# Layer 0's attention: the last four blocks of every second unit's weights turned over on TensorE instead of VectorE

## The chip, the cores and the metric

One core of one Trainium2 chip runs the whole kernel. The metric is device time in microseconds (us), the median of several executions. One more execution was taken with the hardware profiler on; its own time stands beside the others below, and all durations of single instructions come from it.

## The reference, cut to what matters

The kernel computes four layers on an input of 2 x 256 x 32 x 32. Only layer 0 is touched. After a group normalisation it is

```python
q = conv1x1(xn, Wq, bq); k = conv1x1(xn, Wk, bk); v = conv1x1(xn, Wv, bv)   # (2, 32, 32, 256)
qf = q.reshape(8192, 64) / sqrt(64)      # 2048 positions x 4 heads
kf = k.reshape(8192, 64); vf = v.reshape(8192, 64)
A = softmax(qf @ kf.T, axis=1)           # 8192 x 8192: heads share all keys
O = (A @ vf).reshape(2, 32, 32, 256)
x = x + O @ Wo.T + bo
```

All numbers are fp32. Every one of the 8192 queries attends to all 8192 keys, so the matrix of weights is large and never stored. Layers 1 to 3 (another attention, a windowed attention, additive attention, two mixtures of experts) follow and are the same before and after.

## The kernel before, in words

`layer0` normalises, computes `qT`, `kT` and `v`, and calls `shared_attention`. There 64 **rows** are run, each of 32 positions with their 4 heads. A row has 4 **units**: unit `m` belongs to row `i = m // 4`, to the pair of heads `p = m // 2 % 2` and to the half `h = m % 2` of the keys. An odd unit therefore has `h = 1`.

A unit passes through these steps, each a small function:

- `score(m)` (line 143): 16 matmuls (32 in the records, since an fp32 matmul shows as two) into two PSUM tiles, `ps_s0` (two buffers) and `ps_s1` (one buffer). The 128 partitions are 4 groups `c` of 32 queries. The 1024 columns are 32 blocks `b` of 32 keys `i`: partition group `c` and column block `b` meet in the 32 keys `(b, c, i)`. VectorE copies the first tile to `sc0` with a running minimum (line 150, the "eviction" below), ScalarE the second to `sc1` (line 153).
- `fold` (lines 166 to 168, GpSimd) and `reduce` (line 172, VectorE) find the minimum of `sc1`; a gather by DMA (line 159), `spread_least` (line 178 on VectorE) and four more DMAs (line 181) bring each query's minimum to all partitions as `sa_shift`.
- `weigh(m)` (line 188, ScalarE): two exponentials over 128x1024, in place in `sc0` and `sc1`.
- `turn(m)` (line 201, VectorE): two stream transposes over 128x1024. Each turns every 32x32 block on its own, so that in the tile `wt` a block's 128 keys `(c, i)` stand on the partitions and 32 queries in the columns.
- `value(m)` (line 211, TensorE): 16 matmuls (32 records) that multiply `wt` by the rows of `v` and sum into `ps_o`, which has one buffer and holds one row.

At the end of a row `invert`, `spread` (line 230: one matmul into `ps_n`, copied to `norm` by ScalarE, line 235) and `done` (line 372: VectorE multiplies `ps_o` by `norm` into `oT`) normalise it. Every eighth row `done` also runs the output projection, 8 matmuls (16 records) into `ps_out` (line 379), and adds it to `x` on VectorE (line 386). `ps_n` and `ps_out` share one PSUM buffer, the tag `ps_t` of the pool `p_t`.

The order is written out by hand, under `tc.manual_schedule()`: the program order of each engine is the order of the calls. Iteration `n` of the loop calls `reduce(n-2)`, the row's `done`, `turn(n-7)`, `spread_least`, `weigh(n-6)`, `score(n)`, `fold(n)`, the rest of `done` (the projection), `invert`, `spread`, `value(n-10)`, each where its unit or row exists. Engines run freely within that order and meet at semaphores. `sc0` has 7 buffers, so the eviction of unit `n` writes where unit `n-7` stood; `sc1` has 8, `wt` 3.

```python
for n in range(units + 15):
    ...
    if on(7):
        turn(n - 7)
```

Of the kernel before, what the change touches and what calls it, by code (L numbers as in the profile page):

```python
# [19 lines left out]
F32 = mybir.dt.float32  # L20
# [3 lines left out]
ALU = mybir.AluOpType  # L24
# [3 lines left out]
P = 128  # L28
B, C, N = 2, 256, 1024
T = B * N  # L30
NT = T // P
# [38 lines left out]
class Stack:  # L70
# [34 lines left out]

    def shared_attention(self, qT, kT, v, ctx, done):

        tc, nc = self.tc, self.nc
        S, G, B = 32, P // 32, N // 32
        rows = T // S
        units = 4 * rows
        psum = lambda name, bufs: ctx.enter_context(tc.tile_pool(name=name, bufs=bufs, space=PSUM))
        p_a, p_b, p_o, p_t = psum("sa_a", 2), psum("sa_b", 1), psum("sa_o", 1), psum("sa_t", 1)
        sb = ctx.enter_context(tc.tile_pool(name="sa_sb", bufs=2))
        keys = kT.rearrange("p n (b c i) -> p n b c i", c=G, i=S)
        ones = sb.tile([S, P], F32, name="ones", bufs=1)
        nc.gpsimd.memset(ones, 1.0)  # L130
        names = "least folded got shift total parts scores weights sums rec norm"
        least, folded, got, shift, total, parts, scores, weights, sums, rec, norm = ({} for _ in names.split())

        def score(m):
            i, p, h = m // 4, m // 2 % 2, m % 2
            if h == 0:
                least[m // 2] = self.small.tile([P, 2, 2], F32, name="sa_least")
            ps = [pool.tile([P, 2, CH], F32, name=f"ps_s{r}") for r, pool in enumerate((p_a, p_b))]
            for a in range(2):
                for c in range(G):  # L140
                    for r in range(2):
                        half = slice(64 * r, 64 * r + 64)
                        nc.tensor.matmul(  # L143
                            ps[r][S * c : S * (c + 1), a, :].rearrange("p (b i) -> p b i", i=S),
                            lhsT=qT[half, p, S * i : S * (i + 1)], rhs=keys[half, 2 * h + a, :, c, :],
                            start=True, stop=True,
                        )
            scores[m] = [sb.tile([P, N], F32, name=f"sc{r}", bufs=7 + r) for r in range(2)]
            flat = [x.rearrange("p a b -> p (a b)") for x in ps]
            nc.vector.tensor_scalar(  # L150
                scores[m][0], flat[0], 1.0, None, ALU.mult, ALU.min, accum_out=least[m // 2][:, 0, h : h + 1]
            )
            nc.scalar.copy(scores[m][1], flat[1])  # L153

        def gather(t, n, name, engine=nc.sync):

            g = self.small.tile([S, n, G, 2], F32, name=name)
            for c in range(G):
                engine.dma_start(out=g[:, :, c, :], in_=t[S * c : S * (c + 1)])
            return g.rearrange("q n c h -> q n (c h)")  # L160

        def fold(m):
            x = scores[m][1]
            a, b = x[:, :CH], x[:, CH:]
            folded[m] = y = sb.tile([P, CH], F32, name="fold")
            nc.gpsimd.tensor_tensor(y, a, b, ALU.subtract)  # L166
            nc.gpsimd.tensor_scalar(y, y, 3.0e38, 0.0, ALU.min, ALU.max)
            nc.gpsimd.tensor_tensor(y, a, y, ALU.subtract)  # L168

        def reduce(m):  # L170
            h = m % 2
            nc.vector.tensor_reduce(least[m // 2][:, 1, h : h + 1], folded.pop(m), AX.X, ALU.min)
            if h == 1:
                got[m // 2] = gather(least.pop(m // 2), 2, "sa_got")

        def spread_least(k):
            t = self.small.tile([S, 2], F32, name="sa_min")
            nc.vector.tensor_reduce(t, got.pop(k), AX.X, ALU.min)
            shift[k] = self.small.tile([P, 2], F32, name="sa_shift")
            for c in range(G):  # L180
                nc.sync.dma_start(out=shift[k][S * c : S * (c + 1)], in_=t)

        def weigh(m):
            i, p, h = m // 4, m // 2 % 2, m % 2
            if m % 4 == 0:
                total[i] = self.small.tile([P, 4, 2], F32, name="sa_total")
            for r in range(2):
                nc.scalar.activation(  # L188
                    scores[m][r], scores[m][r], AF.Exp, bias=shift[m // 2][:, r : r + 1], scale=-1.0,
                    accum_out=total[i][:, 2 * p + r, h : h + 1],  # L190
                )
            if m % 4 == 3:

                parts[i] = gather(total.pop(i), 4, "sa_sums", nc.sync if i < rows - 3 else nc.scalar)

        def turn(m):
            i, p, h = m // 4, m // 2 % 2, m % 2
            if p == 0:
                weights[i, h] = sb.tile([P, 4, N], F32, name="wt", bufs=3)
            for r, x in enumerate(scores.pop(m)):  # L200
                nc.vector.transpose(weights[i, h][:, 2 * p + r, :], x)  # L201

        def value(m):
            i, h, j = m // 4, m // 2 % 2, m % 2
            if h == 0 and j == 0:
                sums[i] = p_o.tile([P, 4, S], F32, name="ps_o")
            for t in range(B // 4):
                for k in range(2):
                    b = B // 2 * k + B // 4 * j + t
                    at = B * h + b  # L210
                    nc.tensor.matmul(  # L211
                        sums[i][64 * k : 64 * (k + 1)],
                        lhsT=v[:, at % NT, 64 * (at // NT) : 64 * (at // NT + 1)],
                        rhs=weights[i, h][:, :, S * b : S * (b + 1)],
                        start=(h == 0 and j == 0 and t == 0), stop=(h == 1 and j == 1 and t == B // 4 - 1),
                    )

        def invert(i):
            t, r = (self.small.tile([S, 4], F32, name=f"sa_{n}") for n in ("tot", "rec"))
            nc.vector.tensor_reduce(t, parts.pop(i), AX.X, ALU.add)  # L220
            nc.vector.reciprocal(r, t)
            rec[i] = sb.tile([S, 4, S], F32, name="diag")
            shape = [S, 4, S]
            nc.gpsimd.tensor_tensor(
                rec[i], self.ident[0:S, 0:S].unsqueeze(1).to_broadcast(shape), broadcast(r, shape), ALU.mult
            )

        def spread(i):
            ps = p_t.tile([P, 4, S], F32, name="ps_n", tag="ps_t")
            nc.tensor.matmul(  # L230
                ps.rearrange("p n q -> p (n q)"), lhsT=ones, rhs=rec.pop(i).rearrange("p n q -> p (n q)"),
                start=True, stop=True,
            )
            norm[i] = sb.tile([P, 4, S], F32, name="norm")
            nc.scalar.copy(norm[i], ps)

        with tc.manual_schedule():
            for n in range(units + 15):
                on = lambda d: 0 <= n - d < units
                row = lambda d: on(d) and (n - d) % 4 == 0  # L240
                if on(2):
                    reduce(n - 2)
                if row(14):
                    i = (n - 14) // 4
                    ended = done(i, sums.pop(i), norm.pop(i), p_t)
                    next(ended)
                if on(7):
                    turn(n - 7)
                if on(4) and (n - 4) % 2 == 0:
                    spread_least((n - 4) // 2)  # L250
                if on(6):
                    weigh(n - 6)
                if on(0):
                    score(n)
                    fold(n)
                if row(14):
                    next(ended, None)
                    next(ended, None)
                if row(11):
                    invert((n - 11) // 4)  # L260
                if row(13):
                    spread((n - 13) // 4)
                if on(10):
                    value(n - 10)
# [3 lines left out]
    def layer0(self, xT):  # L268
        tc, nc = self.tc, self.nc
        with ExitStack() as ctx:  # L270
# [4 lines left out]
            qT = big.tile([P, CC, T], F32, name="qT")  # L275
            kT = big.tile([P, 4, T], F32, name="kT")
            v = big.tile([P, NT, C], F32, name="v")

            with tc.tile_pool(name="l0_xn", bufs=1) as xp, tc.tile_pool(
                name="l0_ps", bufs=4, space=PSUM  # L280
# [67 lines left out]
                for i in range(NT):  # L348
# [5 lines left out]
                        )  # L354
                    nc.vector.tensor_tensor(v[:, i, :], ps, bv, ALU.add)


            zero = big.tile([P, C], F32, name="zero")
            nc.gpsimd.memset(zero, 0.0)
# [25 lines left out]
                    x = xT[:, o, t * C : (t + 1) * C]  # L385
                    nc.vector.scalar_tensor_tensor(x, ps[:, o, :], bo[:, o : o + 1], x, ALU.add, ALU.add)

            self.shared_attention(qT, kT, v, ctx, done)

    def pool_stats(self, pool, psum, mv, average, tag="ps_row"):  # L390

# [1445 lines left out]
```

## Time and profile before

| what | value |
|---|---|
| median of 3 runs | 2885.95 us (2885.02 to 2887.11) |
| the profiled execution | 2887.74 us, of which the recorded span 2886.0 us |
| mean granted TensorE clock | 0.967; 1.00 in layer 0's attention |
| layer 0's scores | from 62.15 us to about 1130 us |
| busy in the span: TensorE, VectorE, ScalarE, GpSimd | 91%, 67%, 63%, 43% |
| busy from 200 to 1100 us: VectorE, TensorE | 98% to 100%, 96% to 99% in every 100 us |

An engine's busy time is the time in which at least one of its instructions is in flight. Matmul records overlap each other (the mean record of line 211 lasts 276 ns although 32 of them start within 1.9 us), so for TensorE the distance between starts says more than the busy share. "PEld" are weight loads, which have records of their own. In a list of groups the columns are line, engine, operation, output and input, shapes, count, then busy time and mean duration of one, then the engine's idle time just before and what ended it. In a timeline they are start, duration until the end of the merged instructions, engine, line, operation and count, and in brackets the idle time before with what ended it.

### The profile page before, as it was taken

To read this page: it belongs to the slowest core of one execution; us is meant where nothing else is said; L and a number is where in the kernel's file an instruction comes from. 1 tells how busy PE (TensorE), PEld (TensorE's weight loads), DVE (VectorE), ACT (ScalarE), POOL (GpSimd) and SP (SyncE) were. 2 spreads that over 40 slices of the span, in tenths; PEclk is the share of its full clock that TensorE was granted. 3 is DMA by queue.
4 is the path that set the end of the run, shared out by engine and by line. 5 is a ranking of instruction groups with operands and counts; after the bars stand their busy time and mean duration, and the time that the engine had idled before them with its cause. 6 is when DMAs were issued, how large, how long until landed. Compare 5 with 4: busy or idle time off the path is not lost. (4 is left out here: it accounts for less than half of the span.)

```text
span 2886.0 us, 77396 instructions
## 1 busy us (share of the span) xinstructions
PE 2635.3 (91%) x32006; PEld 1643.6 (57%) x32006; DVE 1944.8 (67%) x3642; ACT 1815.6 (63%) x2685; POOL 1235.5 (43%) x1302
## 2 busy tenths in 40 slices
PE   7899999999999998799999686999999988999987
PEld 3455555555555555555555454998666632465676
DVE  5999999999999999478789577633422343134242
ACT  2777777778777777255555231211699878889722
POOL 4877777777777775001111134244111112102242
PEclk9999999999999999899999897999999999899998
DMA  3000000000000000111010100543222001322354
GB/s 133 3 3 3 3 3 3 3 3 3 3 3 3 3 3 3 49 31 28 11 31 9 28 1 30 202 134 99 68 81 76 16 24 35 128 67 87 116 166 125
DMA packets 180577, 131.39 MB, mean 46 GB/s; under 512 B 130992, under 2 KB 162368, under 8 KB 173056
## 3 DMA queue, kind: packets, MB, share of 16 engines
q0 software_dynamic: 29232, 81.71, 8.5%
q1 hardware_dynamic: 147824, 44.25, 6.8%
q8 instruction: 251, 4.11, 0.6%
q10 hardware_dynamic: 3168, 0.48, 0.1%
q14 instruction: 102, 0.84, 0.1%
HBM read 181.24 MB, written 29.49 MB: 73 GB/s over the span
## 5 line engine op out<-in xcount | busy, mean ns | idle before, releaser
L188 ACT ACTIVATE sc<-sc,sa_shift 128x1024 f32<-128x1024 f32 x512 | 584.5, 1144 | 153.1 <-DMA sa_shift<-sa_min 150.8
L201 DVE STREAM_TRANSPOSE wt<-sc 128x1024 f32<-128x1024 f32 x512 | 601.5, 1207 | 0.2 <-ACT sc L188 0.2
L1622 ACT ACTIVATE th<-kT,qb 128x1024 f32<-128x1024 f32 x512 | 540.4, 1135 | 66.2 <-PE ps_e L1631 40.1
L211 PEld LDWEIGHTS ps_o<-wt,v 128*64 128x64 f32 x8192 | 444.4, 137 | 188.9 <-issue 106.2
L143 PE MATMUL ps_s<-kT,qT 64*32 64x512 f32 x8192 | 527.6, 595 | 18.0 <-ACT sc L153 17.2
L211 PE MATMUL ps_o<-wt,v 128*64 128x128 f32 x8192 | 505.0, 276 | 26.8 <-DVE oT L372 26.7
L166 POOL TENSOR_TENSOR fold<-sc 128x512 f32<-128x512 f32 x256 | 329.2, 1286 | 195.9 <-ACT sc L153 177.0
L168 POOL TENSOR_TENSOR fold<-sc,fold 128x512 f32<-128x512 f32 x256 | 328.4, 1283 | 21.4
L153 ACT COPY sc<-ps_s 128x1024 f32<-128x1024 f32 x256 | 256.0, 1000 | 111.0 <-PE ps_s L143 57.1
L1631 PE MATMUL ps_e<-th,pick 128*32 128x512 f32 x2048 | 305.7, 613 | 20.5 <-ACT th L1622 9.3
L1404 PEld LDWEIGHTS ps_h<-xe,ew 128*128 128x128 f32 x2320 | 278.1, 194 | 63.6 <-issue 39.0
L150 DVE TENSOR_SCALAR_CACHE_REDUCE sc<-ps_s 128x1024 f32<-128x1024 f32 x256 | 304.3, 1189 | 7.1 <-PE ps_s L143 6.6
L1404 PE MATMUL ps_h<-xe,ew 128*128 128x128 f32 x2320 | 295.0, 281 | 13.7 <-issue 5.6
L1424 PE MATMUL ps_y<-ew,h 128*128 128x256 f32 x1160 | 275.6, 387 | 8.2 <-ACT h L1410 5.6
L143 PEld LDWEIGHTS ps_s<-kT,qT 64*32 64x32 f32 x8192 | 134.4, 106 | 230.2 <-issue 163.4
L1424 PEld LDWEIGHTS ps_y<-ew,h 128*128 128x128 f32 x1160 | 215.6, 193 | 66.7 <-issue 23.0
L630 ACT ACTIVATE sc<-sc,l_least 128x1024 f32<-128x1024 f32 x128 | 146.7, 1147 | 125.8 <-DVE sc L617 125.5
L1415 DVE TENSOR_TENSOR hb<-ps_h,ew 128x512 f32<-128x512 f32 x115 | 79.4, 691 | 207.3 <-PE ps_h L1404 167.1
L1428 DVE COPY y<-ps_y 128x256 f32<-128x256 f32 x99 | 41.9, 423 | 229.7 <-PE ps_y L1424 209.9
L1393 ACT ACTIVATE h<-hb 128x512 f32<-128x512 f32 x115 | 71.5, 623 | 193.0 <-DVE hb L1415 173.7
L636 DVE STREAM_TRANSPOSE wt<-sc 128x1024 f32<-128x1024 f32 x128 | 153.3, 1225 | 46.0 <-ACT sc L630 25.4
L617 DVE TENSOR_SCALAR_CACHE_REDUCE sc<-ps_s 128x1024 f32<-128x1024 f32 x128 | 150.7, 1213 | 40.3 <-PE ps_s L609 40.2
(286 smaller groups left out, 3139.1 us busy)
## 6 DMA issues: line engine op xcount, KB each, us to landing
xr<-slots_in SPq DMA_DIRECT2D x99, 128.0 KB
slots_out<-y SPq DMA_DIRECT2D x99, 128.0 KB
sa_got<-sa_least SPq DMA_DIRECT2D x512, 0.5 KB
sa_shift<-sa_min SPq DMA_DIRECT2D x512, 0.2 KB
slots_in<-zero POOLq DMA_DIRECT2D x46, 128.0 KB
kh<-kh SPq DMA_DIRECT2D x32, 128.0 KB
qh<-qh SPq DMA_DIRECT2D x32, 128.0 KB
sa_sums<-sa_total SPq DMA_DIRECT2D x244, 1.0 KB
```

The costliest lines, as they stand in the source:

```text
L143: nc.tensor.matmul(ps[r][S * c : S * (c + 1), a, :].rearrange("p (b i) -> p b i", i=S), lhsT=qT[half, p, S * i : S * (i + 1)], rhs=keys[ha ...
L150: nc.vector.tensor_scalar(scores[m][0], flat[0], 1.0, None, ALU.mult, ALU.min, accum_out=least[m // 2][:, 0, h : h + 1])
L153: nc.scalar.copy(scores[m][1], flat[1])
L166: nc.gpsimd.tensor_tensor(y, a, b, ALU.subtract)
L168: nc.gpsimd.tensor_tensor(y, a, y, ALU.subtract)
L188: nc.scalar.activation(scores[m][r], scores[m][r], AF.Exp, bias=shift[m // 2][:, r : r + 1], scale=-1.0, accum_out=total[i][:, 2 * p + r, ...
L201: nc.vector.transpose(weights[i, h][:, 2 * p + r, :], x)
L211: nc.tensor.matmul(sums[i][64 * k : 64 * (k + 1)], lhsT=v[:, at % NT, 64 * (at // NT) : 64 * (at // NT + 1)], rhs=weights[i, h][:, :, S * ...
L1404: nc.tensor.matmul(ps[:, j, :], lhsT=a[:, c, at : at + P], rhs=x[:, c, :], start=(c == 0), stop=(c == CC - 1),)
L1424: nc.tensor.matmul(ps, lhsT=h[:, j, :], rhs=w2[:, j, :], start=(j == 0), stop=(j == HB - 1))
L1622: nc.scalar.activation(h, keys, AF.Tanh, bias=self.qb[b][:, s // G, g : g + 1])
L1631: nc.tensor.matmul(pe[i][c * U : (c + 1) * U, a, :], lhsT=self.pick[:, k, :], rhs=h[:, a, :], start=(k == 0), stop=(k == G - 1),)
```

## The change

For odd units (`h = 1`) VectorE turns only the first 896 of the 1024 columns of each score tile. The last 128 columns, four blocks of 32, are turned by TensorE in the new step `turn_last(m)`: two transposes of 128x128 (one for `sc0`, one for `sc1`) into one PSUM tile `ps_t`, which has the buffer that `ps_n` and `ps_out` use, and one copy by ScalarE into the columns of `wt` that were left out. In iteration `n` it stands behind `score(n)` and `fold(n)`, and ahead of the projection and of `value(n-10)`.

A transpose of a whole 128x128 puts other keys together than four transposes of 32x32 do: the partitions become `(b, i)` of the last four blocks and the 32-column groups become `c`. So the four matmuls of `value` that take these columns need the rows of `v` in that order. They are computed once in `layer0`, as `v_last`: GpSimd copies the normalised inputs into the order (two copies), 8 matmuls (64 columns each) multiply them by the last 64 columns of `wv`, and VectorE adds the bias. `diag` and `norm` go from two buffers to one.

```diff
+    def turn_last(m):
+        i, p, h = m // 4, m // 2 % 2, m % 2
+        both = scores.pop(m)
+        if h == 0:
+            return
+        ps = p_t.tile([P, 2, P], F32, name="ps_t", tag="ps_t")
+        for r, x in enumerate(both):
+            nc.tensor.transpose(ps[:, r, :], x[:, N - P :], self.ident)
+        nc.scalar.copy(weights[i, h][:, 2 * p : 2 * p + 2, N - P :], ps)
 
     def turn(m):
-        for r, x in enumerate(scores.pop(m)):
-            nc.vector.transpose(weights[i, h][:, 2 * p + r, :], x)
+        n = N - h * P
+        for r, x in enumerate(scores[m]):
+            nc.vector.transpose(weights[i, h][:, 2 * p + r, :n], x[:, :n])
...
     def value(m):
-                    lhsT=v[:, at % NT, 64 * (at // NT) : 64 * (at // NT + 1)],
+                    lhsT=v[:, at % NT, 64 * (at // NT) : 64 * (at // NT + 1)]
+                    if h == 0 or b < B - G else v_last[:, b - (B - G), :],
...
-        rec[i] = sb.tile([S, 4, S], F32, name="diag")
+        rec[i] = sb.tile([S, 4, S], F32, name="diag", bufs=1)
-        norm[i] = sb.tile([P, 4, S], F32, name="norm")
+        norm[i] = sb.tile([P, 4, S], F32, name="norm", bufs=1)
...
                 if on(0):
                     score(n)
                     fold(n)
+                if on(7):
+                    turn_last(n - 7)
...
     # layer0, behind the loop that computes v
+    last = xp.tile([P, CC, 4, 4, 32], F32, name="last")
+    runs = xn[:, :, T - 4 * P :].rearrange("p a (b c i) -> p a b c i", b=4, c=4)
+    for c in range(CC):
+        nc.gpsimd.tensor_copy(last[:, c].rearrange("p c b i -> p b c i"), runs[:, c])
+    ps = psum.tile([P, 4, 64], F32, name="ps_v", tag="ps_row")
+    for t in range(4):
+        for c in range(CC):
+            nc.tensor.matmul(
+                ps[:, t, :], lhsT=last[:, c, t].rearrange("p b i -> p (b i)"), rhs=wv[:, c, C - 64 :],
+                start=(c == 0), stop=(c == CC - 1),
+            )
+    nc.vector.tensor_tensor(v_last, ps, bv[:, C - 64 :].unsqueeze(1).to_broadcast([P, 4, 64]), ALU.add)
```

More of the change, by code (lines that the diff above doesn't have):

```diff
@@ L104, in rsqrt, with shared_attention @@
         return r
-    def shared_attention(self, qT, kT, v, ctx, done):
+    def shared_attention(self, qT, kT, v, v_last, ctx, done):
         tc, nc = self.tc, self.nc
@@ L277, in layer0 @@
             v = big.tile([P, NT, C], F32, name="v")
+            v_last = big.tile([P, 4, 64], F32, name="v_last")
             with tc.tile_pool(name="l0_xn", bufs=1) as xp, tc.tile_pool(
@@ L386, in done @@
                     nc.vector.scalar_tensor_tensor(x, ps[:, o, :], bo[:, o : o + 1], x, ALU.add, ALU.add)
-            self.shared_attention(qT, kT, v, ctx, done)
+            self.shared_attention(qT, kT, v, v_last, ctx, done)
     def pool_stats(self, pool, psum, mv, average, tag="ps_row"):
```

## The prediction

> **What bounds the kernel now.** I read the busy times by stretch first, each stretch one group of 8 rows, from the start of a row's first line-211 matmul to that of the eighth row after it.
>
> ```profile
> 235.80:370.00 134.20, 132.81 (x2082) 77.51 (x2082) 133.53 (x202) 104.55 (x167) 103.35 (x104) 1.00 0.06 3
> ...
> 909.40:1043.90 134.50, 131.56 (x2081) 77.54 (x2080) 133.64 (x202) 105.39 (x168) 104.74 (x105) 1.00 0.06 3
> sum 808.10, PE 790.15 PEld 464.44 DVE 801.63 ACT 633.24 POOL 625.93; mean PE 131.69 PEld 77.41 DVE 133.60 ACT 105.54 POOL 104.32
> ```
>
> Columns: length, then busy time of TensorE, its weight loads, VectorE, ScalarE, GpSimd. VectorE works 133.6 of 134.7 us, so it is the bound; ScalarE and GpSimd have 29 us left. TensorE's 131.7 cannot be taken at its word, since its records overlap. The groups of VectorE in this window come next:
>
> ```profile
> L201 DVE STREAM_TRANSPOSE wt<-sc 128x1024 f32<-128x1024 f32 x384 | 451.1, 1207 | 0.0
> L150 DVE TENSOR_SCALAR_CACHE_REDUCE sc<-ps_s 128x1024 f32<-128x1024 f32 x192 | 228.1, 1188 | 0.5
> L172 DVE TENSOR_REDUCE sa_least<-fold 128x1 f32<-128x512 f32 x192 | 127.3, 663 | 0.0
> ```
>
> The last field is idle time: there is none, and the transposes are the largest part. How much room TensorE has is read from starts in its timeline, the rows around a projection:
>
> ```profile
> 631.12 1.97 PE L211 MATMUL ps_o<-wt,v 128*64 128x128 f32 x32
> 633.01 1.95 PE L143 MATMUL ps_s<-kT,qT 64*32 64x512 f32 x32
> 635.98 3.72 PE L379 MATMUL ps_out<-oT,sb_wo 128*128 128x256 f32 x16 [1.02 <-DVE oT L372]
> 639.63 1.97 PE L211 MATMUL ps_o<-wt,v 128*64 128x128 f32 x32
> 641.53 1.95 PE L143 MATMUL ps_s<-kT,qT 64*32 64x512 f32 x32
> 643.41 1.97 PE L211 MATMUL ps_o<-wt,v 128*64 128x128 f32 x32
> ...
> 650.96 0.48 PE L230 MATMUL ps_n<-diag,ones 32*128 32x128 f32 x2
> 651.37 1.97 PE L211 MATMUL ps_o<-wt,v 128*64 128x128 f32 x32
> ```
>
> Back to back, value costs 1.90 us (639.63 to 641.53), score 1.88 (641.53 to 643.41), `ps_n` 0.41, the projection 3.65. So a row on TensorE alone is 4 x 3.78 + 0.41 = 15.53 (15.51 by the rows' starts), and a group 8 x 15.51 + 3.65 = **127.7 us**. The starts of rows in a quiet group show who leads: 20.25 (with the projection), 15.51, 15.51, 16.52, then 16.60 four times, together 134.2. After a projection VectorE has caught up and TensorE sets the pace for two rows; then VectorE falls behind again, its eviction starting 0.2 us after the scores' end in the first unit and about 3 us after it from the tenth on, and rows take 16.6. TensorE's room is 134.2 - 127.7 = 6.5 us a group. That is all that the new work may use.
>
> **The change, part by part.**
>
> *Off VectorE.* A group has 16 odd units, so 32 shorter transposes. By proportion 128 of 1024 columns are 1207/8 = 151 ns; by the slope between 128x512 (663) and 128x1024 (1188) they are (1188 - 663)/4 = 131 ns, different operations but the same engine. I take 0.133: -4.3 us a group (-4.8 at most). VectorE's floor becomes 133.6 - 4.3 = **129.3**. Were nothing else changed, 64 rows would give 34 us.
>
> *Onto TensorE.* 16 pairs of transposes a group. The same operation on fp32 stands at line 1661, here in front of matmuls on part of the columns (128*32), as it will be in front of value (128*64):
>
> ```profile
> 2210.02 1.09 PE L1661 MATMUL ps_pt<-ident,sc_a 128*128 128x128 f32 x8
> 2211.05 1.06 PE L1631 MATMUL ps_e<-th,pick 128*32 128x512 f32 x8
> ```
>
> Eight take 1.03 us from first start to the next operation's start. The single records lie 0.165 (first to second), then 0.109 apart, and 0.20 to the matmul behind; an fp32 transpose is one record, not two. The first does not come later behind tiled scores than value would. A pair is then 0.165 + 0.20 = **0.365 us**. Ends: 0.31 with 0.11 between the two (line 1379, in front of line 1631), and 0.41 by the `ps_n` pair, which has weights and columns of this size, in this very place. Below 0.22 (two steps of 0.109) no row goes. The group grows by 16 x 0.365 = 5.8, to 127.7 + 5.8 = **133.6**. TensorE passes VectorE's 129.3 and becomes the bound.
>
> The Trainium skill, "TensorE: Matmul & The Clock Gate", Part 4, puts a 128x128 transpose at some 275 ns in a kernel's context (bf16). The records here agree as durations (272 ns), but starts lie 0.109 apart. If the page's figure were what a transpose occupies, an estimate from it is 0.55 us a pair, 136.5 us a group and some 20 us slower in all: a rule against this change, which I set aside for the starts.
>
> *Waits added.* First, `ps_t` is one buffer. Transposes wait for the copy of `norm` an iteration earlier, long done. But in the eighth row the projection stands straight behind the transposes and must wait for ScalarE's copy out of the same buffer; behind it on TensorE are value and the next score. ScalarE starts `sc1`'s copy 0.20 us after the scores when it keeps up (seen in the units after a projection), starts the next instruction 0.9 later, and needs 0.37 for 128x256 (between 264 ns for 128 columns and 1000 for 1024); with 0.05 to signal that is 1.52 us after the scores, less the transposes' 0.365: **1.2 us**, up to 2 if ScalarE is as late as now in that unit (0.9 median). It replaces today's wait of 1.0 for `oT`, which goes, because VectorE no longer trails. Second, the eviction in even iterations waits for the first transpose, which is the last reader of `sc0`'s old buffer; `reduce` and two transposes are queued behind it, and score two iterations on waits for it. It is 0.4 us after the scores instead of 0.2, and score two iterations on starts 6 us later: covered. Third, ScalarE gets 16 x 0.37 = 5.9 us a group (105.5 to 111), behind `sc1`'s copy and ahead of the next exponentials. The next score needs only the copy ahead of it. Its cover is the 121 us that line 188 waits for `sa_shift` (1.4 us a time); without it 5.9 a group would be at risk.
>
> *Sum of a group.* 133.6 + 1.2 = 134.8 (unrounded 127.73 + 5.84 + 1.2 = 134.77) against 134.2 quiet: +0.55. By kind of row: the five at 16.6 fall to 16.24, the two at 15.51 rise to 16.24, the one with the projection rises from 20.25 to 21.1. The six groups average 134.7 because of late DMAs; I keep that 0.5 in both. Seven groups and a bit: **+4**. In the first three rows (18.2, 18.0, 15.6) TensorE waits for ScalarE and DMA anyway: nothing.
>
> *Ahead of it.* 16 more records on TensorE behind `v`, at 0.11 apart by the transposes' weight loads: 1.8 us, all on the path, since the first score waits for VectorE's last bias addition (line 143 idle "<-DVE v L355"). With the first step **+1.9**; 0.9 if weights hide. GpSimd's two copies end before, as it idles 29.75 us there. *Behind it* VectorE ends less late (1.1 us behind at the last unit) and turns its last two odd units faster: **-1**. Shorter buffers for `diag` and `norm` cost nothing: each is used again four iterations later. `v_last` in place of `v` has the same shape.
>
> Sum: +4 + 1.9 - 1 = +4.9, say +4.6 with the first fill's cover. The profiled execution goes from 2887.7 to 2892.3; the median, 1.8 below it, from 2885.95 to **2890.5**. The 0.2% that a measurement can tell from no change is 5.8 us: my forecast lies inside it, on the slow side.
>
> **The rivals.**
>
> *Level, as above* (0.63): 0.31 to 0.41 a pair moves a group by -0.9 to +0.7, the projection's wait by -0.5 to +0.8: -3 to +12 us in all. Inside it about 0.42 for within 0.2%, 0.20 above it, 0.01 below.
>
> *Faster: the second weight load and the switch to value hide* (0.12). A pair is then 0.22: 127.7 + 3.5 + 1.2 = 132.4 a group, -1.8, over seven and a half groups -13, +1 for the ends: -12, 2874. For it: eight transposes in a row do run at 0.109. Against: each pair stands alone between tiled matmuls, and every such switch in the trace costs 0.20. VectorE's own floor limits this at about -34 us.
>
> *Slower: the wait for `oT` stays* (0.25). `ps_o` has one buffer; value of a new row waits for VectorE's `oT`. Today it waits 0.7 to 1.0 us in each VectorE-paced row, inside TensorE's room. There will be no room. If VectorE still trails by more than some 1.7 us when a row ends, because ScalarE's longer queue or late shifts hold `turn` back, that wait is paid on top: 16.24 + 0.8 = 17.0 for five rows in eight, against 16.6: +2.2 a group on top of the +0.55, about +20 us with the ends, 2906. For it: two engines within 4% of each other that wait for each other in turn. Against: where TensorE leads today (two rows after a projection) VectorE trails by 0.2 to 1.8 us and no wait shows.
>
> *The change does not do what it says*: the diff and the instruction order leave no room for this; VectorE's odd transposes have 896 columns.
>
> **How the numbers follow.** Faster 0.12 + 0.01 = 0.13; same 0.42; slower 0.25 + 0.20 = 0.45. The level case alone gives 2883 to 2898. To leave out no more than 2 in 10 the range takes in the slower rival's centre and a little below the level case: 2880 to 2906.
>
> **What would show it.** Right: rows of 16.2 us all through a group and one of 21; line 204 (896 columns) near 1075 ns; VectorE with 4 to 5 us of idle time a group, ended by TensorE (scores or `ps_t`); the projection released by ScalarE's copy after 1.2 us; pairs 0.165 and 0.20 apart; the first score near 64.0 us. Wrong: rows still at 16.6 with VectorE never idle (a pair then costs more but does not bind), rows under 16.0 (weights hidden), or a wait for `oT` or for `sc1` on TensorE in every row.

## The result and the profile after

| | before | after |
|---|---|---|
| median, same chip | 2885.02 us (2879.55 to 2888.22, 7 runs) | 2892.02 us (2886.84 to 2896.30, 7 runs) |
| profiled execution, its span | 2887.74 us, 2886.0 us | 2892.02 us, 2890.3 us |
| mean granted TensorE clock | 0.967 | 0.967 |

The ratio is 1.0027, 95% interval 1.0015 to 1.0039: 7.0 us slower, by the interval 4 to 11. The forecast was 4.6 us slower.

Lines of `shared_attention` move down by 2 to 16, those of `done` in `layer0` by 30: score is line 145 now, the eviction 152, ScalarE's copy 155, the exponentials 190, the stream transposes 204, TensorE's transposes 213 and their copy 214, value 224, `ps_n` 244, `oT` 402, the projection 409. The stretches of one group (first value matmul of a row to that of the eighth row after it), columns as before:

```profile
238.20:373.00 134.80, 133.72 (x2115) 79.37 (x2114) 130.21 (x202) 111.13 (x184) 104.50 (x104) 1.00 0.06 3
...
913.20:1048.00 134.80, 133.72 (x2113) 79.37 (x2112) 130.17 (x202) 111.33 (x184) 104.58 (x104) 1.00 0.06 3
sum 809.80, PE 803.31 PEld 476.33 DVE 780.53 ACT 666.29 POOL 627.20; mean PE 133.89 PEld 79.39 DVE 130.09 ACT 111.05 POOL 104.53
```

VectorE works 130.1 us of 135.0 now and has 4.9 us of idle time a group; before it had 1.1. TensorE's busy time went from 131.7 to 133.9. Six groups take 809.8 us where they took 808.1. Most of VectorE's idle time lies in one place. In the list of waits of these six groups (engine and what it was about to write, what it waited for, us in total, times, longest) the addition behind the projection waits for the projection, and TensorE has one kind of wait only:

```profile
DVE xT L416 <- PE ps_out L409: 19.3, 6, 3.5
PE ps_out L409 <- ACT wt L214: 6.5, 6, 1.1
```

So 3.2 of the 4.9 us stand at the projection. In a quiet row without a projection VectorE is idle for 0.12 us (0.58 in the one straight behind it): between projections it is nearly as full as TensorE.

The groups of VectorE in that window, with the two shapes of the transposes apart:

```profile
L204 DVE STREAM_TRANSPOSE wt<-sc 128x1024 f32<-128x1024 f32 x192 | 225.7, 1209 | 0.0
L204 DVE STREAM_TRANSPOSE wt<-sc 128x896 f32<-128x896 f32 x192 | 200.5, 1079 | 0.1
```

A short one lasts 130 ns less. TensorE's timeline around a projection, rows as before:

```profile
621.16 0.44 PE L213 MATMUL ps_t<-ident,sc 128*128 128x128 f32 x2
621.52 1.97 PE L224 MATMUL ps_o<-wt,v 128*64 128x128 f32 x32
623.42 1.95 PE L145 MATMUL ps_s<-kT,qT 64*32 64x512 f32 x32
...
637.40 0.44 PE L213 MATMUL ps_t<-ident,sc 128*128 128x128 f32 x2
638.92 3.72 PE L409 MATMUL ps_out<-oT,sb_wo 128*128 128x256 f32 x16 [1.08 <-ACT wt L214]
642.57 1.97 PE L224 MATMUL ps_o<-wt,v 128*64 128x128 f32 x32
644.47 1.95 PE L145 MATMUL ps_s<-kT,qT 64*32 64x512 f32 x32
```

A pair of transposes takes 0.36 us from its start to that of value (621.16 to 621.52). Value and score keep their 1.90 and 1.88. In the projection's iteration (the lines below the dots) there is a wait: the projection starts 1.52 us after the pair's start, released by ScalarE's copy of `ps_t`. TensorE waits for nothing else in the row, and so the rows of a quiet group are even: 16.25 us seven times, 21.05 once, 134.80 a group, where they were 15.51 twice, 16.52, 16.60 four times and 20.25.

Ahead of the first row, in the timeline:

```profile
61.42 1.89 PE L381 MATMUL ps_v<-sb_wv,last 128*128 128x64 f32 x16
63.36 0.42 DVE L385 TENSOR_TENSOR v_last<-ps_v,sb_bv 128x256 f32<-128x256 f32 x1 [1.31 <-PE ps_v L381]
63.84 2.76 PE L145 MATMUL ps_s<-kT,qT 64*32 64x512 f32 x34 [0.52 <-DVE v_last L385]
```

The first score starts at 63.84 instead of 62.15 us, behind the 16 records for `v_last` and VectorE's addition. When the 64 records for `v` begin differs between executions (46.7 to 48.8 us in the traces of this document), but from there to the first score it is 14.49 us before and 16.22 to 16.23 in all thirteen kernels with `v_last`: 1.74 us.

### The profile page after: what moved, and what is told of

The parts are those of the page before. It is cut to its first block, busy times and chain, and to the rows that moved or that the text cites. A ratio compares the mean times of both kernels' runs of the same rounds, so it can differ in the third digit from the quotient of the medians.

```text
span 2890.3 us, 78147 instructions
## 1 busy us (share of the span) xinstructions
PE 2662.5 (92%) x32278; PEld 1663.7 (58%) x32278; DVE 1916.7 (66%) x3643; ACT 1858.2 (64%) x2813; POOL 1238.7 (43%) x1304
## 5 line engine op out<-in xcount | busy, mean ns | idle before, releaser
L204 DVE STREAM_TRANSPOSE wt<-sc 128x1024 f32<-128x1024 f32 (+1 forms) x512 | 568.3, 1144 | 1.7 <-ACT sc L190 1.6
L145 PE MATMUL ps_s<-kT,qT 64*32 64x512 f32 x8192 | 505.6, 597 | 14.4 <-ACT sc L155 13.8
L170 POOL TENSOR_TENSOR fold<-sc,fold 128x512 f32<-128x512 f32 x256 | 328.3, 1282 | 21.4
L145 PEld LDWEIGHTS ps_s<-kT,qT 64*32 64x32 f32 x8192 | 126.3, 106 | 211.6 <-issue 170.9
L666 DVE STREAM_TRANSPOSE wt<-sc 128x1024 f32<-128x1024 f32 x128 | 153.4, 1225 | 46.0 <-ACT sc L660 25.3
```

What stands on the lines that cost most here:

```text
L145: nc.tensor.matmul(ps[r][S * c : S * (c + 1), a, :].rearrange("p (b i) -> p b i", i=S), lhsT=qT[half, p, S * i : S * (i + 1)], rhs=keys[ha ...
L204: nc.vector.transpose(weights[i, h][:, 2 * p + r, :n], x[:, :n])
```

## The experiments

All ran beside the kernel before, four on one chip at a time: the first four beside 2884.26 us, the next four on a chip where the kernel before takes 2848.64, the last four beside 2887.17. Differences to the kernel before are therefore compared, not times. The third column is the difference of the medians; the ratio is estimated separately and can differ from the quotient of the medians by up to 2 us. Two numbers come from each kernel's trace: the mean group (six groups, projections included) and the **attention's end**, the start of the last matmul into `ps_out`. What lies behind that is the same program in all of them and took 1715 to 1729 us on the first and the third chip, 1675 to 1683 on the second. Each trace is one execution, and the time differences hold that scatter too.

| kernel | ratio to before, 95% | us to before | mean group | attention's end |
|---|---|---|---|---|
| before | | | 134.7 | 1168.3 |
| changed | 1.0027 (1.0015 to 1.0039) | +7.0 | 135.0 | 1173.0 |
| e3_double | 1.0100 (1.0085 to 1.0114) | +28.7 | 138.1 | 1193.5 |
| e4_later | 0.9995 (0.9984 to 1.0006) | -0.9 | 133.7 | 1163.3 |
| e1_vector_all | 1.0129 (1.0115 to 1.0144) | +37.2 | 138.3 | 1202.8 |
| e2_no_transposes | 1.0008 (0.9997 to 1.0019) | +4.3 | 133.3 | 1168.4 |
| e2b_vector_alone | 0.9920 (0.9907 to 0.9934) | -21.4 | 131.9 | 1150.7 |
| e8_vector_filled | 1.0084 (1.0071 to 1.0098) | +24.5 | 136.8 | 1187.8 |
| e5_odd_rows | 0.9976 (0.9958 to 0.9994) | -7.3 | 133.7 | 1163.4 |
| e9_odd_later | 0.9979 (0.9969 to 0.9990) | -4.4 | 133.9 | 1164.9 |
| e10_odd_split | 0.9991 (0.9979 to 1.0003) | -2.2 | 133.9 | 1163.4 |
| e11_split | 1.0018 (1.0006 to 1.0029) | +6.5 | 135.0 | 1170.9 |
| e12_vector_alone_split | 0.9943 (0.9929 to 0.9956) | -14.5 | 131.8 | 1148.6 |
| e13_one_queue | 1.0010 (1.0001 to 1.0019) | +4.6 | 134.8 | 1169.3 |

All diffs below are against the changed kernel.

**Does TensorE set the pace, and what does a transpose cost it?** The first test runs each transpose twice.

```diff
-            for r, x in enumerate(both):
-                nc.tensor.transpose(ps[:, r, :], x[:, N - P :], self.ident)
+            for r, x in enumerate(both + both):
+                nc.tensor.transpose(ps[:, r % 2, :], x[:, N - P :], self.ident)
```

> Each of TensorE's transposes is done twice (four in a row in place of two). Theory (TensorE is the bound and each transpose occupies it for 0.109 us once the first is under way): +0.22 us a pair, rows at 16.25 + 0.44 = 16.7, +3.5 a group, +28 us (2920). Rival (there is room on TensorE, or VectorE sets the pace): 0 to 5 us. If a transpose occupied TensorE for its record's 272 ns: +0.54 a pair, +70 us.

Its TensorE timeline:

```profile
641.08 0.66 PE L213 MATMUL ps_t<-ident,sc 128*128 128x128 f32 x4
641.67 1.97 PE L224 MATMUL ps_o<-wt,v 128*64 128x128 f32 x32
...
651.15 3.72 PE L409 MATMUL ps_out<-oT,sb_wo 128*128 128x256 f32 x16 [0.86 <-ACT wt L214]
```

Four transposes take 0.59 us, two took 0.37: 0.11 for each added one. Rows are 16.69 us, 0.44 above 16.25, which is the four added transposes of a row and nothing else. So every 0.11 us that TensorE gets appears in the time: it is the bound. Only at the projection part of it hides in the wait, which falls from 1.08 to 0.86. Some 22 us over the changed kernel were measured where 28 were expected; by the traces' ends it is 20.5. The expectation had counted 3.5 us for each of eight groups; a mean group grew by 3.1.

The second test moves the projection, which stands straight behind a pair in the changed kernel, into the next iteration, which has none.

```diff
-                if row(14):
+                if row(15):
                     next(ended, None)
                     next(ended, None)
```

> The output projection and its addition move one iteration later, into an odd iteration that has no transposes, so that it no longer stands behind ScalarE's copy out of the shared PSUM buffer. Theory: the 1.15 us that TensorE waits there in each eighth row goes, the row with the projection falls from 21.05 to 19.9, 8 x 1.15 = -9 us against the changed kernel (2883), which is about 2 us under the kernel before. Rival (the wait is hidden or comes back elsewhere, as a wait for the buffer or for the addition): 0 to -3 us.

```profile
636.40 1.95 PE L145 MATMUL ps_s<-kT,qT 64*32 64x512 f32 x32
638.28 3.72 PE L409 MATMUL ps_out<-oT,sb_wo 128*128 128x256 f32 x16
641.93 1.97 PE L224 MATMUL ps_o<-wt,v 128*64 128x128 f32 x32
```

The bracket is gone; the projection starts 1.88 us after the score. Row with projection 19.90 instead of 21.05, group 133.65 instead of 134.80, the attention's end 9.7 us earlier, the time 8 us less: the wait for the shared buffer cost 1.15 us a group on the path, one for one. In its groups the list of waits names none of TensorE.

**What did VectorE's saving bring?** First VectorE turned all columns again, with TensorE's transposes still there.

```diff
-            n = N - h * P
+            n = N
```

> VectorE turns all 1024 columns again; TensorE's transposes and ScalarE's copy stay and overwrite the last 128. This gives VectorE back the 4.3 us a group of 8 rows that the change takes off it, and leaves TensorE as in the changed kernel. Theory (TensorE sets the pace of every row, VectorE is off the path): VectorE's 134.2 a group stays just under TensorE's 134.8, so a group stays at 134.8 to 135.3 and the median is 0 to 5 us above the changed kernel (2892 to 2897). Rival (VectorE's work is still on the path and the transposes cost by another way): +4.3 a group, +33 us in all, near 2925.

It missed, and for a reason that the edit made itself. In its list of waits:

```profile
ACT wt L214 <- DVE sa_min L180: 52.2, 61, 1.5
```

ScalarE's copy writes columns that VectorE now writes too, so it waits for VectorE's transposes of the unit (the releaser is named by what VectorE ended last, the short line 180 behind them). In the changed kernel this wait does not exist. It makes the next exponentials and the projection late: the projection stands 2.0 to 3.2 us behind the pair instead of 1.52, its row takes 22.6 to 24.7. The run says nothing on the question. The next one gives VectorE the same time back as work that nobody waits for.

```diff
                 nc.vector.transpose(weights[i, h][:, 2 * p + r, :n], x[:, :n])
+            if h == 1:
+                unused = self.small.tile([P, 1], F32, name="unused")
+                nc.vector.tensor_reduce(unused, scores[m][0][:, N - P :], AX.X, ALU.min)
```

> The changed kernel, with what the change took off VectorE put back as work that nobody waits for: in each odd unit one more minimum over 128 columns, some 0.27 us (by the slope between 512 columns at 663 ns and the 1024 columns at 1188 ns), behind the two shorter transposes. Unlike the run in which VectorE turned all columns, ScalarE's copy does not wait for it. Theory (TensorE is the bound at 16.25 a row, VectorE with it needs 16.6 a row when it leads): the group lies at 134 to 135.5; rows behind the projection 16.25, later rows up to 16.6 once VectorE has fallen some 3 us behind, the projection row 21 to 22; time 0 to 6 us above the changed kernel, 2892 to 2898. Rival (VectorE is still the bound and its saving carries the changed kernel): all 4.3 us a group come back, 32 us above it, 2924.

Stretches by group, and VectorE's waits in the same six groups:

```profile
sum 820.90, PE 808.97 PEld 478.78 DVE 802.64 ACT 663.42 POOL 628.03; mean PE 134.83 PEld 79.80 DVE 133.77 ACT 110.57 POOL 104.67
```
```profile
DVE xT L419 <- PE ps_out L412: 12.9, 6, 4.0
```

VectorE's busy time is back at 133.8 a group, 3.7 more than in the changed kernel. The group grew by 1.85, half of it. The rows show which half: behind a projection four rows stay at 16.25 (TensorE leads, the added work is free), then VectorE has fallen 2.3 to 2.8 us behind and rows take 16.46, 16.73, 16.73 (the added work counts in full). At the projection VectorE catches up and then waits, 2.2 us a group. So neither theory is right in size: +17.5 us over the changed kernel lies between 0 to 6 and 32. TensorE is the bound in the changed kernel, but VectorE is close behind it: its 4.9 us of idle time were not room for all of 3.7 us of work, since two thirds of them stand at the projection.

The other direction is VectorE's saving alone. The first try took the transposes off TensorE and let ScalarE fill the columns from the untransposed scores (the output is not the reference's in those columns).

```diff
-            ps = p_t.tile([P, 2, P], F32, name="ps_t", tag="ps_t")
             for r, x in enumerate(both):
-                nc.tensor.transpose(ps[:, r, :], x[:, N - P :], self.ident)
-            nc.scalar.copy(weights[i, h][:, 2 * p : 2 * p + 2, N - P :], ps)
+                nc.scalar.copy(weights[i, h][:, 2 * p + r, N - P :], x[:, N - P :])
```

> TensorE's transposes are left out; ScalarE copies the last 128 columns of the odd units from the scores straight into the weights, not turned, so those columns' contribution is not the reference's. VectorE's saving, v_last and ScalarE's extra work stay. Theory: TensorE's floor falls back to 127.7 a group, VectorE at 134.2 - 4.3 = 129.9 sets the pace again: -4.9 a group against the changed kernel, about -36 us (2856), with VectorE 3 us behind the scores again and rows of 16.05. Rival (ScalarE's copy or the order of v is what costs): less than 10 us below the changed kernel.

Groups of ScalarE, and a wait of VectorE's eviction:

```profile
L212 ACT COPY wt<-sc 128x128 f32<-128x128 f32 x192 | 47.7, 297 | 0.0
```
```profile
DVE sc L152 <- ACT wt L212: 12.6, 20, 1.0
```

Two copies of 297 ns are dearer than the one of 377 that they replace, and they read the score tiles that the eviction will overwrite, so VectorE waits for ScalarE, 20 times and 12.6 us in six groups. Again the edit made a wait of its own, and the kernel is no faster than the one before: nothing can be read from it on VectorE's saving. In the second try nobody fills the columns; value reads the four blocks ahead of them instead.

```diff
-            ps = p_t.tile([P, 2, P], F32, name="ps_t", tag="ps_t")
-            for r, x in enumerate(both):
-                nc.tensor.transpose(ps[:, r, :], x[:, N - P :], self.ident)
-            nc.scalar.copy(weights[i, h][:, 2 * p : 2 * p + 2, N - P :], ps)
...
-                        rhs=weights[i, h][:, :, S * b : S * (b + 1)],
+                        rhs=weights[i, h][:, :, S * (b - G * (h == 1 and b >= B - G)) : S * (b - G * (h == 1 and b >= B - G) + 1)],
```

> VectorE's saving alone, without work on any other engine: odd units turn 896 columns, nobody turns the last 128, and value takes the block of columns four places ahead instead (for those columns the output is not the reference's). v_last stays. Theory (VectorE saves 0.133 us a transpose, but cannot use all of it, since it catches up with TensorE while the projection occupies TensorE for 3.65 us and then has nothing to do): rows of 16.07 us where VectorE leads, about 15.5 in the one or two rows behind a projection, a projection row near 19.7; group about 131.2 against 134.2, so 22 us off over seven and a half groups, 1.7 back for v_last: 2862 to 2868 where the kernel before has 2885. Rival (the saving is what the prediction called VectorE's floor, 129.3 a group): 34 off and 1.7 back, 2853. Second rival (VectorE saves next to nothing, and what was gained elsewhere hid it): rows stay at 16.6, 2885 or more.

```profile
sum 791.30, PE 780.35 PEld 461.99 DVE 777.95 ACT 636.88 POOL 626.64; mean PE 130.06 PEld 77.00 DVE 129.66 ACT 106.15 POOL 104.44
```
```profile
DVE sa_min L180 <- DMA sa_got<-sa_least: 6.5, 7, 1.3
DVE xT L412 <- PE ps_out L405: 5.5, 6, 1.5
```

21.4 us off, as the first theory had it; by the attention's end 17.6, with the first score 1.1 us later than before. Where VectorE leads, rows are 16.07. With the changed kernel this splits the change in two: **relieving VectorE brings the attention's end from 1168.3 to 1150.7, and the pairs with ScalarE's copies and the wait at the projection take it back to 1173.0**: -17.6 and +22.3, each from single executions.

VectorE's saving does not come through whole. Its busy time falls by 3.9 us a group, the group by 2.8. In six groups its idle time doubles from 6.5 to 13.3 us; the waits named are the two above, which were 1.4 us (line 178) and 3.2 us (line 386) before.

**Is there a version in between?** Pairs in odd rows only:

```diff
-            n = N - h * P
+            n = N - (P if h == 1 and i % 2 == 1 else 0)
...
-            if h == 0:
+            if h == 0 or not (i % 2 == 1):
                 return
...
-                        if h == 0 or b < B - G else v_last[:, b - (B - G), :],
+                        if h == 0 or b < B - G or not (i % 2 == 1) else v_last[:, b - (B - G), :],
```

> Half of the change: TensorE turns the last four blocks of odd units only in odd rows, 8 pairs a group instead of 16; in even rows VectorE turns all 1024 columns. No pair stands any more ahead of a projection. Theory (a pair costs TensorE 0.37 us, a short transpose saves VectorE 0.133): TensorE 127.7 + 3.0 + 1 for a wait at the projection = 131.7 a group, VectorE 133.6 - 2.1 = 131.5, so 131.5 to 132.2 against 134.2: 15 to 20 us off over seven and a half groups, 1.7 for v_last and up to 1.7 for the last rows back: 2867 to 2873, faster than both kernels. Rival (two engines within a per cent of each other, with uneven rows, wait for each other in turn): 133.5 or more, 2882 to 2890.

```profile
sum 802.00, PE 793.98 PEld 470.98 DVE 790.67 ACT 649.41 POOL 628.53; mean PE 132.33 PEld 78.50 DVE 131.78 ACT 108.24 POOL 104.76
```

VectorE's 131.8 is close to the 131.5 computed, but the group is 133.7. This kernel beats the one before by 7.3 us (interval 2 to 12), and so the changed one too; it is half of the 15 to 20 that the floors promised, and the rival's 133.5 a group is nearer. Its groups take 132.9 to 135.2; the second longest and the longest hold a row of 18.0 and one of 18.1, in which ScalarE waits for a late `sa_shift` (3.2 us in the row from 432 us, 5.2 in that from 965). And TensorE waits for `oT` again, in front of value and of the projection, ten times and 7.0 us in the six groups: the two engines do wait for each other in turn here. Moving the projection one iteration on, as above, adds nothing to this version:

```diff
-                if row(14):
+                if row(15):
                     next(ended, None)
                     next(ended, None)
```

> The run with pairs in odd rows only, and in it the row's normalisation and the projection one iteration later. Theory (what is left at the projection is the wait for oT, 0.7 to 1.0 us a group, and it goes where VectorE has an iteration more): 0 to 7 us below the run without it, 2862 to 2873; the limit is VectorE's 131.5 a group. Rival (a later release of ps_o holds up value of the next row): 5 or more above it.

-4.4 against -7.3 us, with intervals that overlap; the ends of the attention are 1.5 us apart. (Only the projection moved; the normalisation stayed where it was.) No pair stands ahead of the projection here, so there was no wait for the shared buffer to remove.

**What holds VectorE off its floor?** My theory was the projection: it keeps TensorE for 3.65 us, VectorE is 2 to 3 us behind and runs out of work. Three kernels cut the projection into two halves of four matmuls, in two iterations.

```diff
                 if row(14):
                     next(ended, None)
+                if row(15):
+                    next(ended, None)
                     next(ended, None)
...
                         nc.tensor.matmul(
                             ps[:, o, :], lhsT=wo[:, n, o * P : (o + 1) * P], rhs=outs[t][:, n, :],
                             start=(n == 0), stop=(n == 3),
                         )
-                yield
+                    yield
```

> Pairs in odd rows only, and the projection cut in two: four of its eight matmuls in the row's iteration, four in the next one, each ahead of a value. Theory (in the uncut run VectorE needs 131.6 us a group and the group takes 133.0 when quiet, because the projection keeps TensorE for 3.65 us and more, VectorE is at most some 2 to 3 us behind, and so it runs out of work for 1.4 us): two pieces of 1.8 us fit into VectorE's lag, the quiet group falls to 131.6 to 132.0, 7 to 10 us off the uncut run, which lay 7 below the kernel before: 14 to 17 us below the kernel before. Rival (what is lost there are rows in which ScalarE waits for late shifts): the group stays, 5 to 8 below the kernel before.

> The changed kernel (pairs in all rows) with the projection cut in two in the same way. Theory (TensorE is the bound there, VectorE has 4.9 us of idle time a group to spare, so there is nothing to gain from a shorter burst; the first piece still waits 1.15 us for ScalarE's copy): group 134.6 to 135.2, the time within 3 us of the changed kernel, 4 to 10 us above the kernel before. Rival (a shorter burst helps in any case): 10 us below the changed kernel, about 3 below the kernel before.

> The run in which VectorE turns 896 columns and nobody the rest (value reads the four blocks ahead of them, so the output is not the reference's there), with the projection cut in two. Uncut it lay 21 us below the kernel before, with a quiet group of 131.4. Theory (VectorE's need is 129.5 a group; what is above it is the time in which the projection leaves VectorE without work): quiet group 129.5 to 130.2, 9 to 14 us off, 30 to 35 below the kernel before, which is what the prediction called VectorE's limit. Rival (late shifts from DMA hold it): the group stays at 131 or more, 20 to 25 below the kernel before.

Each has the edits of the kernel that it is named after. The theory falls. The mean group is 133.9 with the cut and 133.7 without (odd rows), 131.8 and 131.9 (VectorE alone), 135.0 and 135.0 (all rows). The last pair was expected to be level; the other two were to gain 1 to 1.9 and did not. Two of the times lie outside both ranges set for them (-2.2 and -14.5 us), though the attention ends as early as without the cut (1163.4 and 1163.4) or earlier (1148.6 and 1150.7). The times hold what lies behind the attention as well, on another chip than the uncut versions; why they fall short of that is open. With VectorE alone the projection's two rows are 17.4 to 18.0 and 17.44 instead of 19.7 and 15.5, but VectorE's idle time in six groups stays at 13 us, cut or uncut. It has only changed places, as its waits with the cut show:

```profile
DVE sa_min L180 <- DMA sa_got<-sa_least: 4.6, 7, 1.3
DVE xT L414 <- PE ps_out L407: 3.7, 6, 0.6
DVE wt L204 <- PE ps_o L220: 1.5, 6, 0.3
DVE sc L152 <- PE ps_s L145: 1.3, 2, 0.6
```

What stands first is the gather of the minima arriving late. That this is what holds the last 1 to 2 us a group was not tried and stays open.

**The last rows.** In the last three rows the sums are gathered by DMAs from ScalarE's own queue, before and after the change.

```diff
-                parts[i] = gather(total.pop(i), 4, "sa_sums", nc.sync if i < rows - 3 else nc.scalar)
+                parts[i] = gather(total.pop(i), 4, "sa_sums", nc.sync)
```

> The changed kernel with the gather of the sums (sa_sums) on SyncE's queue in the last three rows too, where it is issued from ScalarE's queue before and after the change. Question: the last three rows took 0.9 us more after the change than before it, where the prediction had them gain. Theory (ScalarE waits 4 us there at that gather, and TensorE and VectorE then wait for ScalarE): rows 61 to 63 lose 1 to 3 us, 1 to 3 below the changed kernel, 4 to 6 above the kernel before. Rival (the queue is not the cause, the gather only lands later on the busier queue): 0 to 4 above the changed kernel, 7 to 11 above the kernel before.

ScalarE in the changed kernel, in its timeline:

```profile
1124.35 3.83 ACTq L161 DMA_DIRECT2D sa_sums<-sa_total  x4
1128.28 1.01 ACT L155 COPY sc<-ps_s 128x1024 f32<-128x1024 f32 x1 [3.96 <-DMA sa_sums<-sa_total]
```

Its instructions for the four DMAs hold ScalarE's queue for 3.83 us, the copy of the scores stands behind them, and that row takes 18.55 us. With SyncE's queue it takes 16.25. But the last row goes from 15.36 to 17.27: there ScalarE waits 4.17 us for a shift, which is queued behind the sums. From row 60 to the attention's end it is 58.4 us instead of 59.9. The time is 2.4 us less, inside the theory's 1 to 3, though the intervals overlap; and the kernel with double transposes, which leaves these DMAs on ScalarE's queue, took 57.6 us for the same stretch. That ScalarE's queue holds up that one row is seen; that it costs time in all is not shown.

## Why the prediction held, and where its parts did not

**The bound changes over.** Predicted: TensorE 133.6, VectorE 129.3, rows of 16.24 throughout and one of 21.1, a group of 134.77. Measured: TensorE's rows 16.25 and 21.05, together 134.80 in a quiet group, and VectorE 130.1. The double transposes show the mechanism: 0.11 us each, all of it in the rows. VectorE's idle time came to the 4 to 5 us a group that were named as a sign, but two thirds of it are ended by the projection, not by scores or `ps_t`.

**The pair.** 0.365 from the records of another layer, 0.37 here. The faster rival (0.22) is out: the switch to value costs its 0.20 in every pair. The Trainium skill, "TensorE: Matmul & The Clock Gate", Part 4, gives a bf16 transpose about 275 ns in a kernel's context; the fp32 record here lasts as long (0.44 us for two of which the second starts 0.165 later), but the doubled transposes occupied TensorE for 0.11 each. By the page's figure as occupancy their rows would have grown by 4 x 0.275 = 1.1 us, an estimate; they grew by 0.44.

**The wait at the projection.** 1.52 us from the scores' end was predicted and measured (637.40 to 638.92), 1.15 beyond the pair. The projection starts 0.05 us after the copy's end, the time that the sum had for the signal. Moving the projection took just that away. In the last rows, though, the shared buffer does what the prediction had ruled out: a pair waits 1.68 us there for ScalarE's copy of `norm`.

**The slower rival** said that value would wait for `oT`, as it did in the six groups before:

```profile
PE ps_o L211 <- DVE oT L372: 13.0, 24, 1.0
```

After the change no such wait of TensorE is left. In most rows VectorE starts its eviction 0.5 to 0.7 us after the scores instead of some 2 to 3, and `oT` is ready 1.76 us before value. After a late gather it trails by up to 2.4 us until the next projection, gaining some 0.2 us a row; even then `oT` is 0.34 us early. So the prediction's limit of some 1.7 us of lag was too low. ScalarE's added work, 5.5 us a group instead of 5.9, cost no time in these rows; its wait for `sa_shift` shrank from 121 us to 19 in the six groups, and its wait for the scores grew instead.

Two prices of the rivals were wrong in the prediction. Today's wait is 0.5 us on average, not 0.7 to 1.0 in each row. And five waits of 0.8 us would have come to 4.0 us a group on top of the +0.55, not 2.2, since the +0.55 already counts the fall of these rows from 16.6 to 16.24: some 35 us in all, near 2921 and outside the range that was to take this rival in. The level case's own bounds are narrow too: with the pair and the projection's wait both at their ends the sum runs from about -6 to +16 us, not -3 to +12.

**VectorE's saving.** 130 ns a transpose for 133. But the sentence that 64 rows would give 34 us if nothing else changed, and with it the limit set for the faster rival, was wrong: VectorE alone ends the attention 17.6 us earlier (19.8 with the projection cut in two), and the times are 21.4 and 14.5 us shorter. The step that failed was to put a floor in the place of a time. At 129.3 VectorE would have to be busy all the time, and small waits that it had no time for before appear as soon as it is faster (6.5 us for gathers and 5.5 at the projection in six groups). Half the change shows the same: 131.8 of work, 133.7 of time.

**The sum was right, three of its terms were not.** From the traces, to the attention's end, +4.6 us:

| stretch | predicted | measured |
|---|---|---|
| to the first score | +1.9 | +1.7 |
| first score to row 3 | 0 | +1.7 (86.6 to 88.3 us) |
| row 3 to row 56 | +3.6 (6.5 groups of 0.55) | +0.8 (895.1 to 895.9) |
| row 56 to row 60 | part of "and a bit" | +0.7 |
| row 60 to the end | -1 | -0.3 (60.2 to 59.9) |

Quiet groups grew by the predicted 0.6 (134.2 to 134.80). But I kept the 0.5 us a group that late DMAs cost before, and after the change they cost 0.17: one row in 48 is irregular, and in four more traces with all pairs (e3_double, e4_later, e11_split, e13_one_queue) none is. A late gather makes VectorE trail, as above, and the rows stay at 16.25. The fill is the opposite miss. Row 3 starts 86.6 us after the first score in the one trace of before; with all pairs it is 86.7 to 88.6 in seven traces, without any pair (VectorE alone) 86.9 and 89.2. So it is no cost that goes with the pairs; how much of it is a difference between single executions stays open. At the end VectorE's shorter lag brought little; a row there waits for ScalarE's DMA instructions, and the pairs for the shared buffer.

That the total came out at 4.6 is therefore partly luck: a fill 1.7 us and an end 0.7 us dearer than forecast and rows some 2 us cheaper cancel. The median moved by 7.0; its interval, 4 to 11, holds 4.6 too.

## What to carry to other kernels

Moving work from the bound engine to one with a little room pays only up to the point where the two cross: here half of the move gained 7 us, all of it lost 7, and all of it without the wait at the projection was level. Cost the receiving engine by the distance of starts including the switch to its neighbour's kind of instruction, look which shared buffer puts a new wait behind it, and check where in the order that wait falls (one iteration later it was free). A floor of busy time is a limit and not a forecast: near it, small waits that were hidden take a per cent or two (here 131.9 us for 129.7 of work, 133.7 for 131.8). And ask where an engine's idle time stands: what is idle at one place in a group is no room for work in every row.

## What the runs showed of the hardware beyond that

- Steady rows of layer 0's attention agree to 0.01 us on every chip used (15.51, 16.25), with a granted clock of 1.00. The rest of the kernel differs by 32 to 53 us between chips (1675 to 1683 us against 1715 to 1729), with a mean clock of 0.969 to 0.974 on the faster chip and 0.962 to 0.969 on the others.
- A transpose of 128x128 in fp32 follows another after 0.11 us when four run in a row, though its record lasts more than twice that.
- Four small DMAs issued one behind the other hold the issuing queue for some microseconds: 2.6 to 3.8 us on ScalarE's queue (three times each in the kernels before and after), 2.5 to 3.7 on SyncE's, 2.5 in the median.
